# K and V of a cross-attention block as block products of two head groups, with another written order

## The chip, the cores and the metric

The kernel runs on one core of one Trainium2 chip. The metric is the device time in microseconds (us); before the change it is 765.32, the median of three runs (764.75 to 765.59). Engines are named as in the profile: PE (TensorE matmul) with its weight loads PEld, DVE (VectorE), ACT (ScalarE), POOL (GpSimd), SP (SyncE, which here only issues DMAs).

## The reference

One transformer block with cross attention, in f32, for 4 batches of 512 tokens, width 512, 16 heads of 32 and an MLP of 2048:

```python
x = layer_norm(hidden_states, ln1_w, ln1_b)
q = (x @ q_w + q_b).reshape(B, LQ, H, HD).transpose(0, 2, 1, 3)
k = (encoder_hidden_states @ k_w + k_b).reshape(B, LK, H, HD).transpose(0, 2, 1, 3)
v = (encoder_hidden_states @ v_w + v_b).reshape(B, LK, H, HD).transpose(0, 2, 1, 3)
scores = jnp.einsum('bhqd,bhkd->bhqk', q, k) * scale
scores = jnp.where(mask, scores, mask_value)
attn = jax.nn.softmax(scores, axis=-1)
out = jnp.einsum('bhqk,bhkd->bhqd', attn, v)
out = out.transpose(0, 2, 1, 3).reshape(B, LQ, D)
out = out @ cproj_w + cproj_b
hidden = out + residual
y = layer_norm(hidden, ln2_w, ln2_b)
y = jax.nn.gelu(y @ fc_w + fc_b, approximate=True)
y = y @ proj_w + proj_b
return residual + y
```

## The kernel before

The sixteen heads of a batch are taken as four groups of four heads; over the four batches there are 16 groups, w = 0 to 15. For each group PE makes K (`prep_k`, L422: four products of 128x512), Q (`prep_q`, L434: the same) and V (`prep_v`, L443: sixteen products of 128x128), each into one of the four accumulator banks of the ring `accs` (L253). ACT copies K and Q out with their bias, V without; POOL adds V's bias.

Then come four steps of 128 queries (qt = 0 to 3). `scores` (u, L458) writes one bank sc for each of the four heads; `exps` (x, L463) takes each bank with one DVE reduction (L469: mask and minimum) and one ACT exponential (L472). So the next u needs the four banks read by the four x before it. `turn` (r, L475) transposes 32x32 blocks on DVE; for each half of the queries `stay` (d, L494, POOL copies) and `exchange` (e, L501, DMAs issued by SP) bring them to the right partitions, and `attend` (a, L509) multiplies with V. `cproj` (c, L390) multiplies with the output weights, DVE adds the residual, POOL adds proj's bias (`prow`) into a second tile `hp`, and POOL issues the store of `hp` to DRAM (L400). The tile h itself is normalised in place for the MLP (`ln_norm`, L347).

The MLP already uses block products. `fc` (f, L574) takes 2x2 blocks of the weights and of y and forms them with seven block products in place of eight: sums of weight blocks by POOL (`w_sums`, L565, into two buffers `wsum`), sums of y by DVE (`y_sums`), and a chain in one bank to which PE adds three further products; between them ACT copies the bank's state (`joins`, L594: four copies of 128x256), and DVE adds the other bank's two halves (one add of 128x512, one of 128x256). proj (P, L703) does the same at two levels, with its sums on DVE (`pt`, `xs`, `gs`), and its results are added to the hidden state that `load_hid` reads back from DRAM (hd, L656; J, L739).

What sets the order is a text, `ORDER` (L61 to L216): each token names a function, its arguments stand behind colons, and each occurrence runs the function up to its next `yield`. Every engine runs its own instructions strictly in that order, and SP its DMA issues too. Weights of K, Q and V have two buffers for each kind (`kqv_w`, L312), taken by even and odd groups. Part of batch 0's MLP is written between the attention steps of groups 6 and later, and so on; all of proj stands behind the last attention step.

## Time and profile before

| | |
|---|---|
| median of three runs | 765.32 us (764.75 to 765.59) |
| the profiled execution: time, span | 765.16 us, 763.4 us |
| busy share of the span | PE 99%, PEld 71%, DVE 78%, ACT 52%, POOL 47% |
| granted TensorE clock | 1.00 of full speed |
| chain that ended last | PE 91%, DVE 3%, DMA 2%, ACT 2% |
| DMA | 157.45 MB, mean 206 GB/s |

Rows of the order of time read "start, length, engine, line, operation, out<-in, shape, xcount [idle before <- who ended it]". A row of groups has, behind the bar, the busy time in us and the mean length of one in ns, then the engine's idle time before it and what ended it. A row of waits reads "who <- on whom: us in total, times, longest". A row of stretches has a stretch, its length, and each engine's busy time in it with the number of its instructions. A product in f32 is two PE passes, so xcounts of PE are twice the products in the code. Lengths of PE rows include the pipeline's end; what a run of passes costs is read from one start to the next.

### The profile page before, as it was taken

How to read it: one execution, taken by the hardware profiler on the slowest of the kernel's cores; microseconds unless marked ns; L12 is line 12 of the kernel's file. 1: busy time of each engine (PE TensorE's matmuls, PEld its weight loads, DVE VectorE, ACT ScalarE, POOL GpSimd, SP SyncE). 2: the span in 40 equal slices, each digit the busy share in tenths (PEclk: the TensorE clock that was granted, in tenths of full speed). 3: DMA queues.
4: the chain of work that ended last, by engine and by line, in shares of the span. 5: the costliest groups of instructions: out<-in, count | busy, mean ns of one | idle time of the engine just before them, and what ended most of it. 6: DMA issues, size and time to landing. Idle time of an engine off the chain costs nothing.

```text
span 763.4 us, 14160 instructions
## 1 busy us (share of the span) xinstructions
PE 755.2 (99%) x4970; PEld 540.4 (71%) x4970; DVE 594.4 (78%) x1199; ACT 399.9 (52%) x948; POOL 359.5 (47%) x391
## 2 busy tenths in 40 slices
PE   9999999999999999999999999999999999999998
PEld 6556555466666556765665676766888999999997
DVE  3799988999778888887778886654778888867862
ACT  2567856446886686857867687741244221111110
POOL 1153744663577467644598656875302023231322
PEclk9999999999999999999999999999999999999999
DMA  8588888677678877478868777888445778589675
GB/s 288 176 228 238 208 213 225 181 218 208 166 215 226 229 249 206 151 202 235 222 185 216 220 241 235 231 261 304 151 139 181 219 207 190 128 193 282 127 145 110
DMA packets 69445, 157.45 MB, mean 206 GB/s; under 512 B 11600, under 2 KB 24272, under 8 KB 67712
## 3 DMA queue, kind: packets, MB, share of 16 engines
q1 hardware_dynamic: 54272, 126.72, 57.3%
q0 software_dynamic: 14960, 29.82, 16.0%
q8 instruction: 39, 0.64, 0.4%
q14 instruction: 30, 0.25, 0.1%
q10 hardware_dynamic: 144, 0.02, 0.0%
HBM read 69.23 MB, written 25.17 MB: 124 GB/s over the span
## 4 chain that ended last, share of the span: by engine, by line
PE 91%; DVE 3%; DMA 2%; ACT 2%; SPq 1%; issue 1%; POOL 0%; DVEq 0%; POOLq 0%; ACTq 0%
PE acc L572 37%; PE sc L572 12%; PE sc L461 8%; PE acc L426 7%; PE acc L438 7%; PE acc L448 7%; PE acc L519 6%; PE acc L393 6%; PE acc L361 2%; SPq L319 1%; DVE ptt L469 1%; DMA gd<-st 1%; ACT ptt L472 1%; PE acc L792 1%; DVE xn L354 0%
## 5 line engine op out<-in xcount | busy, mean ns | idle before, releaser
L472 ACT ACTIVATE ptt<-ptt,mn 128x512 f32<-128x512 f32 x256 | 183.0, 717 | 79.9 <-DVE mn L469 78.9
L469 DVE CUSTOM_DVE_ANT_0 ptt<-sc,mix 128x512 f32<-128x512 f32 x256 | 165.4, 678 | 35.9 <-PE sc L461 28.0
L497 POOL COPY swap<-swap 32x1088 f32<-32x1088 f32 x128 | 140.0, 1094 | 77.5 <-DVE swap L490 58.1
L480 DVE STREAM_TRANSPOSE swap<-ptt 128x1024 f32<-128x1024 f32 x64 | 79.1, 1235 | 9.3 <-ACT ptt L472 3.2
L487 DVE STREAM_TRANSPOSE swap<-ptt 128x1024 f32<-128x1024 f32 x64 | 78.3, 1223 | 0.0
L461 PE MATMUL sc<-pbt 32*128 32x512 f32 x512 | 74.9, 640 | 0.8 <-ACT pbt L440 0.8
L597 ACT COPY xn<-acc 128x128 f32<-128x128 f32 x75 | 18.5, 269 | 103.8 <-PE acc L572 102.8
L597 ACT COPY st<-acc 128x256 f32<-128x256 f32 x96 | 34.4, 368 | 71.2 <-PE acc L572 51.7
L620 POOL DMA_DIRECT2D gd<-st x32 | 23.5, 739 | 90.4 <-ACT st L618 61.8
L572 PE MATMUL acc<-ys,wsum 128*128 128x256 f32 x256 | 63.3, 384 | 1.2 <-ACT st L597 1.2
L448 PEld LDWEIGHTS acc<-ptt,ext 128*128 128x128 f32 x512 | 58.6, 192 | 7.6 <-issue 4.3
L448 PE MATMUL acc<-ptt,ext 128*128 128x128 f32 x512 | 60.7, 277 | 0.0
L519 PE MATMUL acc<-swap,mix 128*32 128x256 f32 x1024 | 60.6, 382 | 0.0
L426 PE MATMUL acc<-ext,ptt 128*128 128x512 f32 x128 | 58.4, 601 | 0.1
L438 PE MATMUL acc<-ext,ptt 128*128 128x512 f32 x128 | 58.5, 600 | 0.0
L572 PE MATMUL acc<-yT,pbt 128*128 128x256 f32 x240 | 57.9, 384 | 0.0
L393 PE MATMUL acc<-mix 128*128 128x512 f32 x128 | 57.7, 599 | 0.0
L572 PEld LDWEIGHTS acc<-ys,wsum 128*128 128x128 f32 x256 | 47.2, 190 | 14.0 <-ACT st L597 5.0
L572 PEld LDWEIGHTS acc<-yT,pbt 128*128 128x128 f32 x240 | 44.6, 190 | 16.4 <-issue 7.4
L519 PEld LDWEIGHTS acc<-swap,mix 128*32 128x32 f32 x1024 | 30.7, 110 | 32.4 <-issue 10.7
L322 DVE TENSOR_TENSOR st<-acc,st 128x512 f32<-128x512 f32 (+1 forms) x48 | 26.3, 547 | 31.1 <-ACT st L597 23.0
L472 ACT ACTIVATION_READ_ACCUMULATOR ptt<-ptt,mn 128x1 f32 x256 | 48.4, 189 | 0.0
(132 smaller groups left out, 1387.3 us busy)
## 6 DMA issues: line engine op xcount, KB each, us to landing
swap<-swap SPq DMA_DIRECT2D x384, 136.0 KB, 3.2
gd<-st POOLq DMA_DIRECT2D x32, 512.0 KB, 4.3
swap<-gd SPq DMA_DIRECT2D x12, 1024.0 KB, 7.5
pbt<-fc_w_dram SPq DMA_DIRECT2D x40, 256.0 KB, 3.7
xn<-x_dram SPq DMA_DIRECT2D x32, 256.0 KB, 4.3
ext<-fc_w_dram SPq DMA_DIRECT2D x24, 256.0 KB, 3.1
swap<-xn POOLq DMA_DIRECT2D x18, 256.0 KB, 5.3
ptt<-k_w_dram SPq DMA_DIRECT2D x16, 256.0 KB, 4.0
```

The lines of the kernel that those rows point to most:

```text
L393: nc.tensor.matmul(acc, oT[:, g, ts(t, P)], wc[:, g, :], start=(g == 0), stop=(g == NG - 1))
L426: nc.tensor.matmul(acc, S["wk", w][:, d, :], eT[:, d, :], start=(d == 0), stop=(d == ND - 1))
L438: nc.tensor.matmul(acc, S["wq", w][:, d, :], xT[:, d, :], start=(d == 0), stop=(d == ND - 1))
L448: nc.tensor.matmul(acc[:, ts(t, P)], eT[:, d, ts(t, P)], S["wv", w][:, d, :], start=(d == 0), stop=(d == ND - 1),)
L461: nc.tensor.matmul(sc[h], S["qT", w][r, ts(qt, P)], S["kT", w][r, :], start=True, stop=True)
L469: nc.vector.tensor_tensor_reduce(out=s, in0=sc[h], in1=mb, scale=1.0, scalar=FMAX, op0=ALU.add, op1=ALU.min, accum_out=mn)
L472: nc.scalar.activation(s, s, AF.Exp, bias=mn, scale=-1.0, accum_out=S["sums", w][:, qt, h : h + 1])
L480: nc.vector.transpose(*two_heads[0])
L487: nc.vector.transpose(*two_heads[1])
L497: nc.gpsimd.tensor_copy(pT[ts(i, HD), i], tb[ts(i, HD), i])
L519: nc.tensor.matmul(av[ts(h, HD), : 2 * P].rearrange(shape, **kw), v[:, t, ts(h, HD)], p[t][h], start=(t == 0), stop=(t == NT - 1),)
L572: nc.tensor.matmul(o, x[:, k], y[:, k], start=(k == 0 and not more), stop=(k == n - 1), skip_group_check=more)
```

## The change

K and V are made for a pair of groups p (groups 2p and 2p+1) at a time by fc's scheme: 2x2 blocks of the two groups' weights and 2x2 blocks of e (the transposed encoder states: two halves of the contraction, two halves of the tokens), seven block products (`kv`), sums of the weights (`kv_sums`, tokens ks and vs, four of 128x256) and of e (`e_sums`, token es, four of 128x512 for each batch) by POOL, and `joins` by ACT and DVE (tokens kj and vj; K's copies carry the bias). Groups 0 and 1 keep K as whole products (pk). V has two pair buffers in place of five single ones. The third sum of e and of the weights overwrites a block of its own input. The buffers of weight sums are a ring of two that K, V, fc and the last weight sums of proj share.

proj's bias is no longer added before the store: the store reads h, and `p_bias` (token pb) adds it by POOL to the hidden state that was read back, behind the attention; `load_row` (lr) loads its row over cproj's bias, which is done by then.

`ORDER` is another text throughout. In it, k:1 to k:4 and v:0 to v:3 stand whole ahead of u:7:0.

```diff
 ORDER = """
-s1:0 s1:0 s1:0 s1:0 r1:0 n1:0 k:0 lf:0:0 v:0 v:0 k:0 wv:2 wq:1 wv:1 k:1 n1:0 n1:0 n1:0 t1:0:1 t1:0:1 t1:0:0 t1:0:3
-  t1:0:0 t1:0:2 t1:0:2 m:0 qb t1:0:3 q:0 q:0
-u:0:0 x:0:0 x:0:0 x:0:0 x:0:0 q:1 r:0:0
-u:0:1 v:1 r:0:0 x:0:1 x:0:1 x:0:1 x:0:1 r:0:1
-u:0:2 r:0:1 r:0:1 x:0:2 v:2 x:0:2 k:1 r:0:1 x:0:2 v:2 x:0:2
...
+s1:0 s1:0 s1:0 s1:0 r1:0 pk:0 es:0 wk:2 pk:0 n1:0 n1:0 n1:0 n1:0 wv:1 wq:1 lx:1 vs:0 pk:1 t1:0:3 t1:0:0 t1:0:1 t1:0:3
+  t1:0:0 t1:0:2 t1:0:1 t1:0:2 q:0 v:0 m:0 qb s1:1 vs:0 vs:0 vs:0 es:0 es:0 es:0 q:0
+u:0:0 vj:0 x:0:0 x:0:0 x:0:0 v:0 x:0:0
+u:0:1 r:0:0 v:0 k:1 vj:0 x:0:1 v:0 x:0:1 pk:1 x:0:1 vj:0 x:0:1 r:0:0 r:0:1
+u:0:2 q:1 x:0:2 r:0:1 vj:0 kj:1 x:0:2 v:0 q:1 x:0:2 x:0:2 vj:0 r:0:1 r:0:1 r:0:2
+u:0:3 x:0:3 x:0:3 x:0:3 vj:0 x:0:3 lx:1 lf:0:0 lx:2 wq:2 lx:1 lx:1 lf:0:1 lf:0:3 wk:3 lc ks:1 m:0 ks:1 ks:1 wv:2 wq:3
+  wv:3 e:0:0 e:0:0 e:0:0 r:0:3 r:0:2 v:1 k:1 k:1
+u:1:0 kj:1 x:1:0 k:1 kj:1 x:1:0 r:0:3 x:1:0 q:3 q:3 vj:1 x:1:0 r:0:3
+u:1:1 ks:1 d:0:0 d:0:0 vs:1 vs:1 vs:1 r:0:3 d:0:1 vs:1 d:0:1 v:1 v:1 s1:1 x:1:1 kj:1 x:1:1 vj:1 k:1 kj:1 v:1 r:1:0
+  vj:1 s1:1 x:1:1 s1:1 x:1:1 r:1:0 r:1:1 kj:1 vj:1 q:2 r1:1 n1:1 n1:1 n1:1 q:2
+u:1:2 vb:0 v:1 a:0:0 wk:4 e:0:1 le:1 e:0:1 e:0:1 wk:5 le:1 le:1 lf:0:3 lh:0 r:1:1 r:1:1 x:1:2 x:1:2 wv:4 le:1 ks:2
+  es:1 vb:0 ks:2 vj:1 x:1:2 n1:1 vj:1 r:1:1 x:1:2
+u:1:3 ks:2 ks:2 es:1 es:1 r:1:2 x:1:3 a:0:0 d:1:0 t1:1:2 k:2 t1:1:1 x:1:3 t1:1:2 x:1:3 a:0:1 x:1:3
+u:2:0 r:1:2 r:1:3 a:0:1 r:1:3 kj:2 x:2:0 x:2:0 r:1:3 x:2:0 t1:1:0 k:2 k:2 kj:2 t1:1:0 t1:1:1 x:2:0
+u:2:1 k:2 t1:1:3 x:2:1 x:2:1 r:1:3 d:1:0 t1:1:3 e:1:0 e:1:0 e:1:0 wv:5 r:2:0 x:2:1 kj:2 d:1:1 vs:2 vs:2 es:1 wq:5 wq:4
+  e:1:1 e:1:1 x:2:1 a:1:0
+u:2:2 e:1:1 r:2:1 q:4 r:2:0 kj:2 x:2:2 x:2:2 x:2:2 r:2:1 k:2 kj:2 r:2:1 x:2:2 a:1:0 r:2:1
+u:2:3 wk:6 wq:6 d:1:1 d:2:0 vs:2 cb:0 vs:2 vb:1 wk:7 ks:3 ks:3 d:2:0 x:2:3 lf:0:2 e:2:0 e:2:0 q:5 wq:7 e:2:0 v:2 x:2:3
+  r:2:2 x:2:3 x:2:3 q:4 r:2:3 kj:2
...
     mix = const.tile([P, 33 * D // 2], F32, tag="mix", name="mix")
-    v_of = [mix[:, i * D : (i + 1) * D].rearrange("p (t f) -> p t f", t=NT) for i in range(5)]
-    mb = mix[:, 5 * D : 6 * D]
-    rr = mix[:, 6 * D : 6 * D + D // 2].rearrange("p (a h d) -> p a h d", a=2, h=HG)
-    wc, oT = (mix[:, 13 * D // 2 + i * ND * D : 13 * D // 2 + (i + 1) * ND * D].rearrange("p (d n) -> p d n", d=ND)
+    v_of = [mix[:, i * 2 * D : (i + 1) * 2 * D] for i in range(2)]
+    mb = mix[:, 4 * D : 5 * D]
+    rr = mix[:, 5 * D : 5 * D + D // 2].rearrange("p (a h d) -> p a h d", a=2, h=HG)
+    wc, oT = (mix[:, 11 * D // 2 + i * ND * D : 11 * D // 2 + (i + 1) * ND * D].rearrange("p (d n) -> p d n", d=ND)
               for i in range(2))
-    prow, hp = (mix[:, 29 * D // 2 + i * D : 29 * D // 2 + (i + 1) * D] for i in range(2))
+    es = mix[:, 27 * D // 2 : 33 * D // 2].rearrange("p (s i l) -> p s i l", s=3, i=2)
...
     yT = const.tile([P, ND, L], F32, tag="yT", name="yT")
     ys = const.tile([P, 3, 2, HL], F32, tag="ys", name="ys")
-    wsum = const.tile([P, 2, 3, 2, P], F32, tag="wsum", name="wsum")
+    wsums = Ring(const.tile([P, 3, 2, P], F32, tag=f"ws{i}", name=f"ws{i}") for i in range(2))
...
     def k_q(w, i):
-        n = w % 4 * 2 + i
-        return pbt[:, n * D : (n + 1) * D]
+        n = w // 2 % 2 * 4 + i * 2 + w % 2
+        return pbt[:, n * D : (n + 2 - i) * D]
...
         add(nc.vector, h, acc, h)
         accs.done("c", b, t)
         yield
-        add(nc.gpsimd, hp, h, prow)
-        nc.gpsimd.dma_start(out=xa[b][ts(t, P), :], in_=hp)
+        nc.gpsimd.dma_start(out=xa[b][ts(t, P), :], in_=h)
...
         return take
+    def bias(name, w):
+        k = {"k": KB, "q": QB}[name] + w % NG
+        return vec[:, k : k + 1]
+
     def prep_k(w):
-        kT = S["kT", w] = k_q(w, 0)
+
         acc = accs.take("k", w)
         for d in range(ND):
             nc.tensor.matmul(acc, S["wk", w][:, d, :], eT[:, d, :], start=(d == 0), stop=(d == ND - 1))
         yield
-        nc.scalar.activation(kT, acc, AF.Identity, bias=vec[:, KB + w % NG : KB + w % NG + 1], scale=1.0)
+        kT = S["kT", w] = k_q(w // 2 * 2, 0)[:, w % 2 * D : (w % 2 + 1) * D]
+        nc.scalar.activation(kT, acc, AF.Identity, bias=bias("k", w), scale=1.0)
         accs.done("k", w)
+
+    def e_blocks():
+        return [eT[:, 2 * k : 2 * k + 2, j * HL : (j + 1) * HL] for k in range(2) for j in range(2)]
+
+    def e_sums(b):
+        e = e_blocks()
+        return b_sums(nc.gpsimd, *e, es[:, 0], es[:, 1], e[1], es[:, 2])
+
+    def kv_sums(name):
+        def take(p):
+            a = [kqv_w(2 * p + i, "kqv".index(name)) for i in range(2)]
+            s = S["s" + name, p] = wsums.take(name, p)
+            return a_sums(nc.gpsimd, a[0][:, :2], a[0][:, 2:], a[1][:, :2], a[1][:, 2:], s[:, 0], s[:, 1], a[1][:, :2], s[:, 2])
+
+        return take
+
+    def kv(name):
+
+
+        def product(o, x, y, more=False):
+            for t in range(2 if name == "v" else 1):
+                for k in range(2):
+                    i, j = (y[:, k, ts(t, P)], x[:, k]) if name == "v" else (x[:, k], y[:, k])
+                    out_ = o[:, ts(t, P)] if name == "v" else o
+                    nc.tensor.matmul(out_, i, j, start=(k + t == 0 and not more), stop=(k == 1), skip_group_check=more or t > 0)
+
+        def take(p):
+            a, b = [kqv_w(2 * p + i, "kqv".index(name)) for i in range(2)]
+            e11, t3, e21, e22 = e_blocks()
+            t1, t2, t4 = (es[:, i] for i in range(3))
+            chain = S["qa", name, p] = accs.take("qa", name, p)[:, :HL]
+            product(chain, a[:, :2], e11)
+            yield
+            s = S["s" + name, p]
+            q = S["qc", name, p] = halves(accs.take("qc", name, p))
+            product(q[:, 0], a[:, 2:], e21)
+            product(q[:, 1], b[:, :2], t3)
+            yield
+            product(chain, s[:, 1], t2, True)
+            yield
+            product(chain, s[:, 0], t1, True)
+            yield
+            product(chain, s[:, 2], e22, True)
+            product(q[:, 1], b[:, 2:], t4, True)
+            wsums.done(name, p)
+
+        return take
+
+    def k_join(p):
+        kT = k_q(2 * p, 0)
+        for i in range(2):
+            S["kT", 2 * p + i] = kT[:, i * D : (i + 1) * D]
+        b = [bias("k", 2 * p + i) for i in range(2)]
+        return joins(kT.rearrange("p (i n) -> p i n", i=4), ("k", p), True, (b[0], b[0], b[1], b[1]))
+
+    def v_join(p):
+        v = v_of[p % 2]
+        for i in range(2):
+            S["v", 2 * p + i] = v[:, i * D : (i + 1) * D].rearrange("p (t f) -> p t f", t=NT)
+        return joins(v.rearrange("p (i n) -> p i n", i=4), ("v", p), True)
+
+    def v_bias(p):
+        for w in (2 * p, 2 * p + 1):
+            add(nc.gpsimd, S["v", w], S["v", w], row[:, 1, ts(w % NG, P)][:, None, :].broadcast_to([P, NT, P]))
+            yield
     def q_bias():
         nc.vector.tensor_scalar(qb, vec[:, QB : QB + NG], 0.0, -scale, ALU.add, ALU.mult)
...
         yield
         nc.scalar.activation(qT, acc, AF.Identity, bias=qb[:, w % NG : w % NG + 1], scale=-scale)
         accs.done("q", w)
-
-    def prep_v(w):
-        v = S["v", w] = v_of[w % 5]
-        acc = accs.take("v", w)
-        for t in range(NT):
-            for d in range(ND):
-                nc.tensor.matmul(
-                    acc[:, ts(t, P)], eT[:, d, ts(t, P)], S["wv", w][:, d, :],
-                    start=(d == 0), stop=(d == ND - 1),
-                )
-        yield
-        nc.scalar.copy(v, acc.rearrange("p (t f) -> p t f", t=NT))
-        accs.done("v", w)
-        yield
-        add(nc.gpsimd, v, v, row[:, 1, ts(w % NG, P)][:, None, :].broadcast_to([P, NT, P]))
...
         return [mlp_w(2 * (b * NP + c) + i) for i in range(2)]
     def fc_s(b, c):
-        s = wsum[:, c % 2]
+        s = S["sf", b, c]
         return s[:, 0], s[:, 1], fc_w(b, c)[1][:, :2], s[:, 2]
     def w_sums(engine, b, c):
         x, y = fc_w(b, c)
+        S["sf", b, c] = wsums.take("f", b, c)
         return a_sums(engine, x[:, :2], x[:, 2:], y[:, :2], y[:, 2:], *fc_s(b, c))
...
     def fc(b, c):
         a = fc_w(b, c)
         y11, t3, y21, y22 = y_blocks()
         t1, t2, t4 = (ys[:, i] for i in range(3))
-        s1, s2, s3, s4 = fc_s(b, c)
-
         chain = S["qa", b, c] = accs.take("qa", b, c)[:, :HL]
         product(chain, a[0][:, 0:2], y11)
         yield
+        s1, s2, s3, s4 = fc_s(b, c)
         q = S["qc", b, c] = halves(sc[c % HG] if b == LAST else accs.take("qc", b, c))
         product(q[:, 0], a[0][:, 2:4], y21)
         product(q[:, 1], s3, t3)
...
         yield
         product(chain, s4, y22, True)
         product(q[:, 1], a[1][:, 2:4], t4, True)
-
-    def joins(g, key, own):
+        wsums.done("f", b, c)
+
+    def joins(g, key, own, biases=None):
+
+        def copy(i):
+            if biases is None:
+                nc.scalar.copy(g[:, i], S["qa", *key])
+            else:
+                nc.scalar.activation(g[:, i], S["qa", *key], AF.Identity, bias=biases[i], scale=1.0)
         for i in (0, 2, 3):
-            nc.scalar.copy(g[:, i], S["qa", *key])
+            copy(i)
             yield
         q = S["qc", *key]
         add(nc.vector, g[:, 0:4:3], q, g[:, 0:4:3])
         yield
-        nc.scalar.copy(g[:, 1], S["qa", *key])
+        copy(1)
         accs.done("qa", *key)
         yield
         add(nc.vector, g[:, 2], q[:, 1], g[:, 2])
...
     def load_hid(b):
         for t in range(NT):
             load(hids[b % 2][:, t], xa[b][ts(t, P), :])
+            yield
+
+    def load_row():
+        load(row[:, 0, :], rows[1:2, :].broadcast_to([P, D]))
+
+    def p_bias(b):
+        for t in range(NT):
+            o = hids[b % 2][:, t]
+            add(nc.gpsimd, o, o, row[:, 0, :])
             yield
...
         nc.tensor.matmul(warm[:, :P], ident, ident, start=True, stop=True)
     accs.done("warm")
     load(row, rows[None, ::2, :].broadcast_to([P, 2, D]))
-    load(prow, rows[1:2, :].broadcast_to([P, D]))
     load_mask(0, nc.sync)
     takes = {
         "wk": load_k, "wq": load_q, "wv": load_v, "le": load_enc, "lc": lambda: load(wc, c_w),
-        "k": prep_k, "q": prep_q, "v": prep_v, "qb": q_bias, "m": make_mb,
+        "pk": prep_k, "q": prep_q, "es": e_sums, "k": kv("k"), "v": kv("v"), "ks": kv_sums("k"), "vs": kv_sums("v"),
+        "kj": k_join, "vj": v_join, "vb": v_bias, "lr": load_row, "pb": p_bias, "qb": q_bias, "m": make_mb,
...
```

The last weight sums of proj (pt:2) go through the ring in five subtractions in place of four. What is cut from the diff renames places in shared tiles.

More of the change, by code (lines that the diff above doesn't have):

```diff
@@ L571, in product @@
         for k in range(n):
-            nc.tensor.matmul(o, x[:, k], y[:, k], start=(k == 0 and not more), stop=(k == n - 1), skip_group_check=more)
+            w = y[k] if isinstance(y, list) else y[:, k]
+            nc.tensor.matmul(o, x[:, k], w, start=(k == 0 and not more), stop=(k == n - 1), skip_group_check=more)
     def fc(b, c):
@@ L686, in p_terms, with p_sums_split @@
         b11, b12, b21, b22 = quarters(p_of(n))
-        s = ws[n]
-        return (b11, b12, b21, b22), (s[:, 0], s[:, 1], ws3 if n == 4 else b12, s[:, 2])
-    def p_sums2(n):
-        b, t = p_terms(n)
-        return b_sums(nc.vector, *b, *t)
+        if n == 2:
+            t = [S["t2", i] for i in range(2)]
+            t1, t2 = ([w.rearrange("p s i n -> p (s i) n")[:, :4] for w in t])
+            t4 = [w[:, 2, i] for w in t for i in range(2)]
+        else:
+            t1, t2, t4 = ws[n]
+        return (b11, b12, b21, b22), (t1, t2, ws3 if n == 4 else b12, t4)
+    def p_sums2(n):
+        if n != 2:
+            b, t = p_terms(n)
+            return b_sums(nc.vector, *b, *t)
+        for i in range(2):
+            S["t2", i] = wsums.take("t2", i)
+        return p_sums_split()
+    def p_sums_split():
+        (b11, b12, b21, b22), (t1, t2, t3, _) = p_terms(2)
+        sub(nc.vector, t1, b12, b11)
+        yield
+        sub(nc.vector, t2, b22, t1)
+        yield
+        sub(nc.vector, t3, b22, b12)
+        yield
+        for i in range(2):
+            c = slice(2 * i, 2 * i + 2)
+            sub(nc.vector, S["t2", i][:, 2], b21[:, c], t2[:, c])
     def g_terms(b, n):
```

295 lines of the change are left out of this document (145 added, 150 removed).

## The prediction

> **What bounds the kernel now.** I read the page first, then the waits of PE and DVE, then the busy time by stretch, then the order of time for the prices.
>
> ```profile
> PE 755.2 (99%) x4970; PEld 540.4 (71%) x4970; DVE 594.4 (78%) x1199; ACT 399.9 (52%) x948; POOL 359.5 (47%) x391
> ...
> PE acc L792 <- POOL nhalf L781: 1.3, 1, 1.3
> PE acc L572 <- ACT st L597: 1.2, 1, 1.2
> PE acc L361 <- DVE xn L354: 1.0, 1, 1.0
> PE sc L461 <- ACT pbt L440: 0.8, 1, 0.8
> ```
>
> PE has no room: the list of its waits names 4.3 us in all. So time goes where PE's work goes, as long as no other engine takes over. The other engine to watch is DVE, and it must be read by stretch: from the first scores (u:0:0, 22.4) to those of group 7 (u:7:0, 198.9), from there to 490.0 (group 15's last scores), and behind.
>
> ```profile
> core 0: us, PE busy (x) PEld busy (x) DVE busy (x) ACT busy (x) POOL busy (x), PEclk, DMA share, GB/s
> 22.40:198.90 176.50, 175.39 (x1146) 96.88 (x1147) 162.25 (x357) 112.69 (x282) 88.09 (x90) 1.00 0.76 206
> 198.90:490.00 291.10, 289.75 (x1772) 183.73 (x1768) 233.90 (x501) 217.38 (x468) 187.11 (x211) 1.00 0.76 217
> 490.00:763.40 273.40, 269.82 (x1969) 245.98 (x1968) 191.09 (x325) 65.28 (x194) 82.29 (x83) 1.00 0.70 190
> ```
>
> The clock is full throughout (1.00). In the first stretch DVE is busy 162.25 of 176.50, 91.9%; in the second 80%, in the third 70%. In the first it is already nearly a second bound, because each scores group needs the four sc banks that DVE's reductions empty, and there is little MLP work yet to put between.
>
> **The change part by part.** The products of K and V. Prices are from start to start:
>
> ```profile
> 237.74 1.03 PE L572 MATMUL acc<-yT,wsum 128*128 128x256 f32 x4
> 238.60 1.03 PE L572 MATMUL acc<-ys,pbt 128*128 128x256 f32 x4
> ...
> 262.75 3.60 PE L426 MATMUL acc<-ext,ptt 128*128 128x512 f32 x8
> 266.18 1.03 PE L572 MATMUL acc<-ys,wsum 128*128 128x256 f32 x4
> ...
> 292.30 3.72 PE L572 MATMUL acc<-yT,pbt 128*128 128x256 f32 x16
> 295.85 1.03 PE L572 MATMUL acc<-ys,wsum 128*128 128x256 f32 x4
> ...
> 307.24 3.73 PE L448 MATMUL acc<-ptt,ext 128*128 128x128 f32 x32
> 310.81 3.60 PE L426 MATMUL acc<-ext,ptt 128*128 128x512 f32 x8
> ```
>
> A product stands in the trace as two passes. K of one group is 8 passes of 512 columns, 266.18 - 262.75 = 3.43, a pair 6.86. The new pair is 7 blocks of 2 products, 28 passes of 256 columns: at 238.60 - 237.74 = 0.86 for four that is 6.02, at 3.55 for sixteen 6.21. Seven of the eight pairs change (groups 0 and 1 keep whole products): -5.9, at worst -4.6. V of one group is 32 passes of 128 columns, 3.57, a pair 7.14; the new pair has 56, 6.25: -0.89 for each of 8 pairs, -7.1. Together **-13.0**. Each pair is issued in 5 runs in place of 2; the 64 scores groups stay as many, so I cost the breaks at nothing. If each of the 45 added runs paid 0.1 (what 16 passes in a row have over four times 0.86), -13.0 would be -8.5.
>
> ```profile
> L572 PEld LDWEIGHTS acc<-yT,pbt 128*128 128x128 f32 x240 | 44.6, 190 | 16.4 <-issue 7.4 <-ACT st L597 1.5 <-ACT st L618 0.8
> ```
>
> The new K has 196 passes, each with a load of 190 ns, where 112 stood: 84 more. The sixteen passes in 3.55, 222 ns each, already hold a load of 190 each, so loads hide beneath passes and I count nothing. The Trainium skill (TensorE: Matmul & The Clock Gate, Part 3, "What overlaps and what doesn't") says that a weight load runs beside matmuls in flight only if it goes to other row groups. These loads and passes all use the full 128 rows, so by that rule the 84 would add 16.0 and K would lose 10 instead of gaining 5.9; the trace differs, with 222 ns where load and pass one behind the other would take over 400.
>
> The head. What stands ahead of u:0:0 is set by x: its load, its statistics, the four normalisations of L354, transposes, q.
>
> ```profile
> 8.99 3.73 PE L448 MATMUL acc<-ptt,ext 128*128 128x128 f32 x32
> ...
> 12.56 3.60 PE L426 MATMUL acc<-ext,ptt 128*128 128x512 f32 x8
> ...
> 13.76 1.92 DVE L354 TENSOR_SCALAR xn<-xn,mv,rs 128x512 f32<-128x512 f32 x4 [1.45 <-POOL rs L341]
> ...
> 15.99 2.16 PE L361 MATMUL acc<-ident,xn 128*128 128x128 f32 x16
> ...
> 22.38 1.14 PE L461 MATMUL sc<-pbt 32*128 32x512 f32 x8 [0.78 <-ACT pbt L440]
> ```
>
> Before, V of group 0 (8.99 to 12.56) fills the wait. The new order has only V's first block there, 8 passes, 0.9; the other 2.7 is PE work that was free and now stands behind u:0:0: **+2.7**. The second K follows the first and may wait for its weights, but it is covered: before, it was done at 16.2, just as the transposes began.
>
> Beside it, POOL. After rs it was idle; now 8 sums of e and V stand there (four of 128x512, four of 128x256).
>
> ```profile
> 161.12 1.39 DVE L354 TENSOR_SCALAR xn<-xn,mv,rs 128x512 f32<-128x512 f32 x1
> 161.47 0.74 POOL L325 TENSOR_TENSOR wsum<-pbt,wsum 128x256 f32<-128x256 f32 x1
> 163.27 1.27 POOL L322 TENSOR_TENSOR mix<-xn,mix 128x512 f32<-128x512 f32 x1 [1.06 <-DMA xa<-mix]
> 163.37 1.45 DVE L354 TENSOR_SCALAR xn<-xn,mv,rs 128x512 f32<-128x512 f32 x1
> ```
>
> With POOL idle four of L354 take 1.92; beside a POOL sum one takes 1.39 to 1.45, as if it waited for the sum to end. On the head's chain that is 0 (sums late because their V weights land late) up to 4 x 0.9 = 3.6; I take **+2.0**, above the middle, since the sum of e needs no late load and begins as L354 does.
>
> The joins and the first stretch. Each of 15 products now ends in a join like fc's: four copies by ACT and two adds by DVE.
>
> ```profile
> L597 ACT COPY st<-acc 128x256 f32<-128x256 f32 x96 | 34.4, 368 | 71.2 <-PE acc L572 51.7 <-DMA gd<-st 19.4
> L428 ACT ACTIVATE pbt<-acc,vec 128x512 f32<-128x512 f32 x16 | 10.8, 677 | 7.1 <-PE acc L426 7.1
> L453 ACT COPY mix<-acc 128x512 f32<-128x512 f32 x16 | 9.1, 573 | 14.7 <-PE acc L448 14.6
> L322 DVE TENSOR_TENSOR st<-acc,st 128x512 f32<-128x512 f32 x24 | 16.4, 682 | 23.0 <-ACT st L597 23.0
> L322 DVE TENSOR_TENSOR st<-acc,st 128x256 f32<-128x256 f32 x24 | 9.9, 412 | 8.1 <-PE acc L572 8.1
> 24.15 0.69 DVE L469 CUSTOM_DVE_ANT_0 ptt<-sc,mix 128x512 f32<-128x512 f32 x1
> 24.76 0.69 DVE L469 CUSTOM_DVE_ANT_0 ptt<-sc,mix 128x512 f32<-128x512 f32 x1
> ```
>
> ACT: 4 x 0.368 = 1.47 a pair for 2 x 0.677 or 2 x 0.573; 15 pairs add some 3 us to an engine at 52%: nothing. DVE had no part in K and V. Instructions on it start 0.08 before the last ends (0.69 long, 0.61 apart), so a join costs 0.68 + 0.41 less 0.16, 0.94, and 15 cost 14. Behind u:7:0 DVE has 20% free and they cost nothing. Ahead of u:7:0 the new order has four K and four V pairs: PE's work there falls by 4 x 0.84 + 4 x 0.89 = 7.0, 176.5 to 169.5; DVE's rises by 8 x 0.94 = 7.5, 162.25 to 169.8. (Other work crosses the two ends, V of pair 4 to behind and MLP products to ahead; counted in the written order it about cancels on both engines.) DVE would have to be busy without a gap. Nothing in the trace shows it so over a long stretch; the largest of its waits there is this:
>
> ```profile
> DVE ptt L469 <- PE sc L461: 8.4, 8, 4.1
> ```
>
> As it falls behind PE, the 8.4 of waits for scores should go, and what is left of them all is a few us. Ends: 100% gives 169.8, +0.3 over PE's 169.5; the old 91.9% gives 184.8, +15.3. I take 97%, 175.0, **+5.5**, nearer the busy end because the largest wait is one that a late DVE doesn't have.
>
> PE's wait for a join: the third to fifth run adds to a bank that ACT must have copied first. fc has the same chain 32 times and PE waited 1.2 in all; 15 more, **+0.6** (0 to 15 x 1.2 = 18 if every one cost fc's longest).
>
> POOL: 60 sums for K and V and 16 for e.
>
> ```profile
> L325 POOL TENSOR_TENSOR wsum<-wsum,pbt 128x256 f32<-128x256 f32 x20 | 14.8, 746 | 0.2
> L322 POOL TENSOR_TENSOR mix<-xn,mix 128x512 f32<-128x512 f32 x16 | 20.5, 1284 | 25.8 <-issue 9.4 <-DMA xa<-mix 9.2 <-DVE xn L322 7.0
> SPq L319 <- PE acc L426: 10.2, 5, 7.6
> ptt<-k_w_dram SPq DMA_DIRECT2D x16, 256.0 KB, 4.0
> xa<-mix POOLq DMA_DIRECT2D x16, 256.0 KB, 3.3
> ```
>
> 60 x 0.746 + 16 x 1.284 = 65, so POOL goes from 359.5 to 424, 56%: nothing, at its share. If that cover fails (group 1 holds most: its sums and stays), what is late next is stay, then attend. proj's bias: the 16 adds of 1.284 leave the attention, where cproj's store waited for them, and come back behind it, where POOL is busy 82.29 of 273.40: nothing; uncovered in the last batch, 4 x 1.284 = 5.1. proj's row is loaded later by one DMA on SP in place of one in the head: nothing. But the store now reads h itself, which the normalisation overwrites in place, so DVE's first one of a batch waits until the store has landed, 3.3, with the reductions queued behind it and PE's scores behind those. Statistics (two steps) and POOL's rs stand between, so I take nothing; uncovered in all four batches it is 13.
>
> SP: a pair now uses both weight buffers of its kind, so the next pair's two loads wait for its last run, and the exchange DMAs queue behind them. A pair then needs its loads (4.0) and four sums (3.0) before the products, 7 us out of the 50 that two of the first seven groups take (176.5 x 2/7): nothing; if half of 7 pairs showed it, 25. Both sum buffers are shared with fc's sums in the same manner.
>
> The sum, against the profiled execution (765.16, span 763.4; the median of three is 765.32): 765.2 - 13.0 + 2.7 + 2.0 + 5.5 + 0.6 = **763.0**.
>
> **The rivals.** (a) DVE does not bind: the joins fit in its waits. Then +5.5 goes and 757.5 is left, without the contention in the head 755.5. For it: DVE's waits for scores vanish when it is late. Against: 169.8 of work in 169.5.
> (b) DVE keeps its old share in the first stretch, because its waits for ACT's exponentials and for transposes' buffers stay: 184.8, the time 772.8, slower. It decides at one point: 765.2 is reached at a stretch of 177.2, 169.8 / 177.2 = 95.8% busy; beneath 94.9% the kernel is slower by over 0.2%. For it: the row of 91.9%. Against: that row is of a DVE that waits for PE.
> (c) The change does not do what it says: PE's products shrink, but PE waits as long as they shrank, in the head and the first stretch (DVE at 95 to 96.5%): 764 to 766.9.
> (d) Loads of weights no longer hide: 16.0 more, 779. The sixteen passes in 3.55 speak against it.
>
> **How the numbers follow.** Over 0.2% (1.5 us) is what a measurement of this kernel can tell from no change. My forecast, 763.0 with 758 to 763.7 as its own range: 0.38. (a) 0.12. (c) 0.15. (b) 0.33. (d) 0.02. Faster is the forecast and (a), 0.50; the same (c), 0.15; slower (b) and (d), 0.35. The range of 8 in 10 runs from (a) without contention, 755.5, to just under (b), 772.5.
>
> **What would show it.** Right: L524 (scores) of u:7:0 starts some 5 us after a PE-bound 22 + 169.5, DVE busy 96 to 98% between; PE's list of waits gains scores that wait for DVE in that stretch and little behind it; u:0:0 starts near 24.5 with L363 longer than 0.54 each; passes of L467 keep 0.11 and 0.215. Wrong: waits of PE for ACT's copies or POOL's sums of many us, SP queued behind weights, or DVE under 95%.

## The result, and the profile after

The changed kernel takes 778.84 us (median of 777.04 to 780.34), against 765.04 for the kernel before on the same chip: a ratio of 1.0175, with a 95% interval of 1.0158 to 1.0193. Slower, and outside the range of the prediction (755.5 to 772.5). The profiled execution took 780.34, 1.5 above that median, with a span of 778.3, 14.9 more than the 763.4 of before.

The page of the changed kernel, busy time and granted clock in 40 slices:

```profile
PE 757.7 (97%) x4990; PEld 555.0 (71%) x4990; DVE 635.0 (82%) x1230; ACT 404.4 (52%) x978; POOL 426.6 (55%) x467
...
PEclk8999999999999999999999999999999999999999
```

PE was at 99% of the span and is at 97%. POOL stands where it was expected (424 predicted). DVE has 40.6 more than the 594.4 of before, and the joins explain some 14 of that (the forecast's price). So something else has made DVE's work longer. Busy time by the same three stretches (first scores, scores of group 7, last scores of group 15, end), changed kernel:

```profile
core 0: us, PE busy (x) PEld busy (x) DVE busy (x) ACT busy (x) POOL busy (x), PEclk, DMA share, GB/s
25.20:198.50 173.30, 171.52 (x1149) 101.95 (x1148) 165.81 (x371) 119.35 (x302) 115.88 (x128) 1.00 0.79 215
198.50:484.40 285.90, 285.39 (x1772) 187.96 (x1768) 239.12 (x509) 212.86 (x480) 196.66 (x224) 1.00 0.77 216
484.40:778.30 293.90, 280.39 (x2017) 253.41 (x2016) 219.68 (x332) 68.08 (x193) 104.08 (x99) 0.99 0.65 180
```

Against before (22.4, 176.5, 291.1, 273.4) the opening is 2.8 longer, the first stretch 3.2 shorter, the second 5.2 shorter, and the last 20.5 longer. The loss is behind attention, where none of the products that were changed runs; 5.3 of the 20.5 there is work of PE that the new order moved (worked out below), the rest is loss. PE's waits in the changed kernel, from the list of the whole span:

```profile
PE sc L637 <- DVE ext L334: 3.9, 1, 3.9
PE acc L438 <- DMA ptt<-k_w_dram: 3.5, 1, 3.5
PE sc L637 <- DVE xn L331: 2.1, 1, 2.1
PE sc L637 <- DVE st L331: 1.9, 1, 1.9
PE acc L893 <- POOL nhalf L882: 1.3, 1, 1.3
PE acc L637 <- DVE ws L334: 0.9, 1, 0.9
PE acc L637 <- DVE ext L334: 0.7, 2, 0.5
```

Five lines name DVE's additions and subtractions behind attention (9.5 us); before, the longest wait of PE was 1.3 and none was for these. The sums themselves, grouped by line and shape behind 484, changed kernel first (columns: count, then busy time and mean ns of one):

```profile
L334 DVE TENSOR_TENSOR ext<-swap 128x512 f32<-128x512 f32 x25 | 24.5, 985 | 0.0
L334 DVE TENSOR_TENSOR ext<-ext,swap 128x512 f32<-128x512 f32 x25 | 23.9, 958 | 0.7 <-PE sc L637 0.7
```

and the same sums before, behind 490:

```profile
L325 DVE TENSOR_TENSOR ext<-ext,swap 128x512 f32<-128x512 f32 x25 | 17.0, 684 | 0.1
L325 DVE TENSOR_TENSOR ext<-swap 128x512 f32<-128x512 f32 x25 | 17.0, 683 | 0.0
```

In these two groups the same instruction on the same shape takes 0.97 in the mean where it took 0.68. The longest of them, in order of time, changed kernel, DVE, POOL and PE:

```profile
694.23 5.00 DVE L334 TENSOR_TENSOR ext<-swap 128x512 f32<-128x512 f32 x1
...
694.49 1.72 POOL L331 TENSOR_TENSOR swap<-swap,row 128x512 f32<-128x512 f32 x1
695.70 1.67 POOL L849 DMA_DIRECT2D yT<-xn  x1
696.48 2.18 POOL L331 TENSOR_TENSOR swap<-swap,row 128x512 f32<-128x512 f32 x1
...
694.31 1.06 PE L637 MATMUL sc<-pbt,swap 128*128 128x128 f32 x8
699.28 1.16 PE L637 MATMUL sc<-pbt,ext 128*128 128x128 f32 x8 [3.92 <-DVE ext L334]
```

A subtraction of DVE lasts 5.00 us, from before the first bias addition of GpSimd (swap<-swap,row) until 0.57 behind the end of the second, and PE stands for 3.92 until it is done.

I counted DVE's instructions in the trace of the changed kernel: those with no GpSimd instruction beside them (DMA issues left aside), and those with a GpSimd addition at some moment of them (number, mean us, longest us). Those beside GpSimd's copies alone are in neither column.

```
                                            no GpSimd beside        beside an addition
two SBUF inputs, 128x512, add/subtract      146   0.686   0.697     21  1.909  5.000
two SBUF inputs, 128x256                     24   0.420   0.426      2  1.652  1.810
one PSUM, one SBUF input, 128x512            20   0.687   0.692     29  0.675  0.694
scores' reduction (PSUM, SBUF), 128x512      68   0.678   0.693    114  0.678  0.694
32x32 transposes, 128x1024                   25   1.224   1.246     68  1.225  1.246
normalisation (one SBUF input), 128x512      15   0.546   0.603      6  0.908  1.487
```

So GpSimd's additions do nothing to DVE's work in attention (PSUM inputs, transposes), and hold up the additions with two SBUF inputs, of which the projection's sums consist. The Trainium skill (SBUF — State Buffer, "Who interferes with whom") says that a DVE instruction with two SBUF inputs contends with a GpSimd instruction that reads SBUF, over a shared pair of ports that is an exclusive lock, and that issue order decides who blocks. The table agrees in that the rows with two SBUF inputs are hit and those with a PSUM input and the transposes are not; the normalisation, with one SBUF input, is hit as well. Two things in the row at 694.23 go beyond this rule. The subtraction was held over two GpSimd additions and not let in between them (so were those at 592.18 and 738.05, of 4.71 and 3.45; one at 726.83, of 3.85, was let in behind the first). And its record starts 0.26 ahead of the first of the two, which it yet gave way to; since GpSimd's records are rough, the trace can't tell which was issued first.

### The profile page after: what moved, and what is told of

The parts are those of the page before. It is cut to its first block, busy times and chain, and to the rows that moved or that the text cites. A ratio compares the mean times of both kernels' runs of the same rounds, so it can differ in the third digit from the quotient of the medians.

```text
span 778.3 us, 14426 instructions
## 1 busy us (share of the span) xinstructions
PE 757.7 (97%) x4990; PEld 555.0 (71%) x4990; DVE 635.0 (82%) x1230; ACT 404.4 (52%) x978; POOL 426.6 (55%) x467
## 4 chain that ended last, share of the span: by engine, by line
PE 69%; DVE 12%; issue 5%; DMA 5%; POOL 4%; ACT 2%; SPq 2%; DVEq 0%; POOLq 0%; ACTq 0%
PE acc L637 27%; PE sc L637 9%; PE acc L467 9%; PE sc L524 7%; PE acc L516 6%; PE acc L582 5%; PE acc L402 5%; SPq L328 2%; DVE ext L334 2%; DVE ptt L532 2%; DVE swap L543 1%; PE acc L370 1%; POOL swap L560 1%; DMA swap<-swap 1%; PE acc L438 1%
## 5 line engine op out<-in xcount | busy, mean ns | idle before, releaser
L663 ACT COPY st<-acc 128x256 f32<-128x256 f32 x128 | 46.0, 367 | 103.2 <-PE acc L637 84.3
L663 ACT COPY xn<-acc 128x128 f32<-128x128 f32 x100 | 23.5, 269 | 136.5 <-PE acc L637 134.5
L524 PE MATMUL sc<-pbt 32*128 32x512 f32 x512 | 78.0, 640 | 0.0
L691 POOL DMA_DIRECT2D gd<-st x32 | 23.7, 741 | 90.7 <-ACT st L689 56.9
L637 PE MATMUL acc<-ys,ws 128*128 128x256 f32 x256 | 65.4, 386 | 0.8 <-ACT st L663 0.7
L637 PEld LDWEIGHTS acc<-ys,ws 128*128 128x128 f32 x256 | 46.7, 190 | 18.2 <-issue 4.8
L516 PE MATMUL acc<-ext,ptt 128*128 128x512 f32 x128 | 58.4, 599 | 0.0
L849 POOL DMA_DIRECT2D swap<-xn x18 | 22.4, 1423 | 50.0 <-ACT xn L663 18.9
L689 ACT ACTIVATE st<-st,vec 128x512 f32<-128x512 f32 x64 | 43.6, 717 | 3.1 <-DVE st L331 2.7
L516 PEld LDWEIGHTS acc<-ext,ptt 128*128 128x128 f32 x128 | 23.5, 190 | 28.6 <-issue 23.5
L402 PEld LDWEIGHTS acc<-mix 128*128 128x128 f32 x128 | 23.6, 190 | 28.4 <-issue 26.3
```

Source lines behind the costliest of these rows:

```text
L402: nc.tensor.matmul(acc, oT[:, g, ts(t, P)], wc[:, g, :], start=(g == 0), stop=(g == NG - 1))
L516: nc.tensor.matmul(acc, S["wq", w][:, d, :], xT[:, d, :], start=(d == 0), stop=(d == ND - 1))
L524: nc.tensor.matmul(sc[h], S["qT", w][r, ts(qt, P)], S["kT", w][r, :], start=True, stop=True)
L637: nc.tensor.matmul(o, x[:, k], w, start=(k == 0 and not more), stop=(k == n - 1), skip_group_check=more)
L663: nc.scalar.copy(g[:, i], S["qa", *key])
```

## The experiments

The theories. A: the moved bias additions hold DVE up, by contention. B: they cost because the biased rows are now waited for (a load, an addition and then the joins, one behind the other). C: the new products of K and V, and the written order around them, lose the time. In the diffs below, a minus is the kernel named.

**The bias left out.** From the changed kernel:

```diff
-            add(nc.gpsimd, o, o, row[:, 0, :])
             yield
```

> The changed kernel without the 16 POOL adds of proj's bias behind the attention (the bias is left out of the result); the order and everything else stay. Theory A, the two engines' port: a DVE add or subtraction with both inputs in SBUF and a POOL add with both inputs in SBUF do not run side by side, so the 16 adds hold up DVE's sums and through them PE; without them the last stretch falls from 294 to about 279 and the time from 778.8 to about 765. Theory B, waiting in line: POOL's accumulating DMAs of proj's results stand behind adds that wait for the read-back of the hidden state; also about 765 here. Theory C, the written order of the last stretch itself (shared ring of sums, more MLP behind the attention): 777 to 779, no change.

Measured: 766.37 us, ratio to before 1.0019 [1.0000, 1.0039]. The last stretch takes 279.0 in place of 293.9. 12.5 of the 13.8 us are the 16 additions; C is left with the rest. A and B both forecast about 765 here, so this run doesn't part them.

**The bias added by VectorE.**

```diff
-            add(nc.gpsimd, o, o, row[:, 0, :])
+            add(nc.vector, o, o, row[:, 0, :])
```

> The changed kernel with the 16 adds of proj's bias made by DVE in place of POOL, at the same places of the order. Theory A: no POOL add is left to shut DVE out; DVE gets 16 x 0.61 = 9.8 more work in a stretch where it has room; about 766 to 769. Theory B: the accumulating DMAs no longer stand behind the adds on POOL, but DVE now waits for the read-back, with its sums queued behind: 770 to 778. Theory C: 777 to 780.

Measured: 766.03, ratio 1.0014 [0.9999, 1.0029]. The same rows, waited for in the same way, cost nothing that can be measured once VectorE adds them, although VectorE now has 16 more instructions. The two groups of sums that took 0.97 are back at 0.69 in this kernel, behind 484:

```profile
L334 DVE TENSOR_TENSOR ext<-ext,swap 128x512 f32<-128x512 f32 x25 | 17.1, 687 | 2.5 <-PE sc L637 2.5
L334 DVE TENSOR_TENSOR ext<-swap 128x512 f32<-128x512 f32 x25 | 17.1, 686 | 0.0
```

**The additions on GpSimd, on a tile that nobody waits for.** From the changed kernel, bias left out:

```diff
-            add(nc.gpsimd, o, o, row[:, 0, :])
+            add(nc.gpsimd, row[:, 1, :], row[:, 1, :], row[:, 0, :])
```

> The changed kernel with POOL's 16 adds at the same places, but onto a tile that nothing waits for (the row of V's bias, which is done by then), so they wait for no read-back and no accumulating DMA waits for their result; proj's bias is thus left out of the result. POOL's time and its two SBUF inputs stay. Theory A: the adds still shut DVE out, 774 to 779. Theory B: the waiting in line is gone, about 765 to 767. Theory C: 777 to 779.

Measured: 770.81, ratio 1.0080 [1.0057, 1.0102], between the forecasts of A and B. Contention alone costs 4.4 to 4.8 against the two kernels above; PE waits for DVE's sums up to 1.4 at a time, in place of 3.9. The 8 us up to the changed kernel come with the real rows: the additions then start when the rows land, and so beside other instructions of DVE. Whether the 8 is waiting in line or worse moments of contention, this run can't tell.

**The move alone.** The kernel before, with only proj's bias moved behind attention: `hp` and `prow` go, cproj's store reads h, `load_row` and `p_bias` are the changed kernel's, and their tokens (`lr`, sixteen `pb`) are added to an `ORDER` that otherwise stays:

```diff
-        add(nc.gpsimd, hp, h, prow)
-        nc.gpsimd.dma_start(out=xa[b][ts(t, P), :], in_=hp)
+        nc.gpsimd.dma_start(out=xa[b][ts(t, P), :], in_=h)
...
+            add(nc.gpsimd, o, o, row[:, 0, :])
```

> The kernel before with this part of the change alone: the store takes h itself, POOL's 16 adds of proj's bias stand behind the attention, each some 30 tokens behind the load of its tile. Theory A: DVE's sums of two SBUF inputs are shut out 16 times, of which a half to two thirds reach PE: 772 to 778 against 765.0. Theory B: 765 to 772, as far as the adds wait for loads. Theory C: 765 to 766.

Measured: 779.11, ratio 1.0178 [1.0162, 1.0194]. The move by itself, with the old products of K and V, makes as large a loss as the whole change (a little over A's range).

**The same additions aside, in the kernel before.** First on `hp`:

```diff
+    def p_aside(b):
+        for t in range(NT):
+            add(nc.gpsimd, hp, hp, prow)
+            yield
```

> The kernel before, with proj's bias where it was, and 16 more GpSimd additions of 128x512 on a tile that nobody reads, at the places behind attention where the changed kernel has its bias additions. Nothing waits for them and nothing else changes. Theory A, GpSimd shuts VectorE's two-operand additions out while it runs: 768.5 to 771, VectorE's additions there up to 2.5 us each, and the projection waits for them. Theory B, it is only the waiting in line for the biased rows that costs: 765 to 766, as before.

Measured: 777.82. It settles nothing: behind attention the space of `hp` and `prow` holds weight sums of the projection, so the additions changed those, waited for them and were waited for. Again, on the free half of the row tile:

```diff
-            add(nc.gpsimd, hp, hp, prow)
+            add(nc.gpsimd, row[:, 1, :], row[:, 1, :], row[:, 0, :])
```

> The kernel before with the same 16 GpSimd additions of 128x512 at the places behind attention, now on the second half of the row tile, which nobody reads there; the tile of the run before this one (777.82) turned out to be in use by the projection's sums, so that the additions held these up and were held up. Theory A, GpSimd shuts VectorE's two-operand additions out while it runs: 768.5 to 771.5, VectorE's additions there up to 2.5 us each. Theory B, only waiting in line for the biased rows costs: 765 to 766.5, as before.

Measured: 778.73, ratio 1.0169 [1.0144, 1.0195], far above what either theory was given. Sixteen additions that nobody reads cost as much as the moved bias (779.11): here waiting for rows has no part, and B falls. PE's waits and DVE's slowest group behind 484 of this kernel:

```profile
PE acc L574 <- DVE ext L327: 5.6, 2, 2.9
PE sc L574 <- DVE ext L327: 3.5, 3, 2.0
...
L327 DVE TENSOR_TENSOR ext<-swap,ext 128x512 f32<-128x512 f32 x25 | 21.8, 874 | 1.5 <-PE acc L574 1.3
```

The price was thought to be that of the run aside in the changed kernel, and is three times as large. The two kernels are written in another order; the same 16 additions, of 1.7 each, met other sums of DVE. The last stretch of the kernel without bias, of the run aside in the changed kernel, and of this one:

```profile
486.40:765.40 279.00, 275.08 (x2017) 250.03 (x2016) 194.86 (x332) 68.10 (x193) 81.26 (x83) 1.00 0.69 188
```

```profile
484.90:769.00 284.10, 276.35 (x2017) 250.04 (x2016) 213.20 (x332) 68.05 (x193) 103.93 (x99) 1.00 0.68 186
```

```profile
490.70:776.40 285.70, 273.00 (x1969) 247.76 (x1968) 208.38 (x325) 65.33 (x194) 105.78 (x99) 0.99 0.66 182
```

DVE is held up about as much in both: its busy time grows by 18.3 there (194.86 to 213.20) and by 17.3 here (191.09 before, 208.38). But PE's listed waits for DVE come to 3.9 there and 9.1 here. So what an addition costs depends on whether PE soon needs the sum that it meets, and isn't a constant.

**Each bias addition cut in four.** From the changed kernel:

```diff
-            add(nc.gpsimd, o, o, row[:, 0, :])
+            for i in range(4):
+                add(nc.gpsimd, o[:, ts(i, P)], o[:, ts(i, P)], row[:, 0, ts(i, P)])
```

> The changed kernel (778.84) with each of the 16 GpSimd bias additions of 128x512 cut in four of 128x128, in the same places. Theory L, a VectorE addition is shut out for as long as the GpSimd instruction that it met lasts: VectorE's additions meet pieces of 0.35 to 0.45 us, its longest fall from 5.0 us to under 2, and the time falls to 771 to 775. Theory S, the two share one path and what counts is the bytes that GpSimd moves: the longest stay above 3 us, and the time is 777.5 to 781, no better for the 48 more instructions.

Measured: 768.75, ratio 1.0039 [1.0015, 1.0062]: 10 us faster than the changed kernel, more than either theory gave, with the same bytes, the same places, and 48 more instructions on GpSimd (POOL is busy 119.00 of the last stretch in place of 104.08). So it isn't bytes, nor GpSimd's queue. And since the real rows are waited for here as in the changed kernel, waiting in line can hardly be more than 2.4 (768.75 less 766.37) of the 8 us that the run aside left open; the rest points to contention. DVE's 128x512 additions with two SBUF inputs that meet a GpSimd addition take 0.949 in the mean (31 of them), not 1.909. But the picture of one piece at a time is not exact either; the longest is 2.94 (a 128x1024, 1.22 alone), and this one of 128x256 (0.42 alone) waits through all four pieces, DVE and POOL in order of time:

```profile
565.38 2.22 DVE L334 TENSOR_TENSOR ws<-ws,ext 128x256 f32<-128x256 f32 x1
565.54 1.76 POOL L331 TENSOR_TENSOR swap<-swap,row 128x128 f32<-128x128 f32 x4
567.52 0.41 DVE L331 TENSOR_TENSOR ws<-ext 128x256 f32<-128x256 f32 x1
```

**The joins' additions left out.** From the kernel with the bias on VectorE, for the part that is left to C:

```diff
-        add(nc.vector, g[:, 0:4:3], q, g[:, 0:4:3])
+        if not kv_:
+            add(nc.vector, g[:, 0:4:3], q, g[:, 0:4:3])
...
-        add(nc.vector, g[:, 2], q[:, 1], g[:, 2])
+        if not kv_:
+            add(nc.vector, g[:, 2], q[:, 1], g[:, 2])
```

> The kernel with proj's bias added by VectorE (766.03), without the two VectorE additions of each of the K and V joins: the second and third blocks of K and V lack their cross products. It takes some 14 us of work off VectorE and nothing off TensorE. Theory D, VectorE bounds the first stretch of attention (the prediction's third step): that stretch falls from 175.4 to 169 to 171 and the time to 760.5 to 762.5. Theory W, the gain of the K/V part went into a handful of separate waits of TensorE (weights, layer norm, ScalarE's copies of the joins), and its scores never wait for VectorE: that stretch falls by at most 1.5, the time is 764.5 to 766.5.

Measured: 765.72, ratio 1.0008 [0.9986, 1.0029], 0.3 from its base and within its noise. The first stretch, of the base and of this kernel:

```profile
23.70:199.10 175.40, 171.91 (x1147) 102.26 (x1147) 166.00 (x371) 119.69 (x302) 116.09 (x128) 1.00 0.79 213
```

```profile
23.70:195.70 172.00, 170.62 (x1149) 101.52 (x1148) 159.15 (x355) 118.80 (x302) 115.80 (x128) 1.00 0.79 217
```

DVE has 6.85 less to do and the stretch is 3.4 shorter (1.8 against the run without bias, whose stretch is 173.8), between the two forecasts; the time followed theory W. (The additions left out go into the first, third and fourth of the four blocks, not the second and third.) DVE slows that stretch in part, but doesn't bound it: it falls to 92.5% busy and the rest stays. Theory W isn't right to the letter either. Scores do wait for DVE inside their runs, where the list of waits doesn't see it: in the changed kernel four of the 28 groups of scores in this stretch take 1.82 to 2.11 from their first pass to the end of their last, most of the others 1.14.

```profile
114.68 1.14 PE L524 MATMUL sc<-pbt 32*128 32x512 f32 x8
119.38 2.11 PE L524 MATMUL sc<-pbt 32*128 32x512 f32 x8
```

From start to next pass that is some 2 us more over the stretch than before, where two groups are long.

**The opening.** In the changed kernel's opening, DVE and PE in order of time, the second K waits for weights:

```profile
4.91 3.61 PE L438 MATMUL acc<-ext,ptt 128*128 128x512 f32 x8
11.98 6.71 PE L438 MATMUL acc<-ext,ptt 128*128 128x512 f32 x8 [3.47 <-DMA ptt<-k_w_dram]
18.53 2.13 PE L370 MATMUL acc<-ident,xn 128*128 128x128 f32 x16
...
13.76 3.67 DVE L363 TENSOR_SCALAR xn<-xn,mv,rs 128x512 f32<-128x512 f32 x4 [1.45 <-POOL rs L350]
```

Its eight passes take 6.71 in place of 3.61: over 8 to 20 us the granted clock is 0.72. So the loads were put in another order, from the kernel with the bias on VectorE:

```diff
     load_k(0)
...
+    load_k(1)
     load_v(0)
     for _ in load_x((1, 0)):
         pass
-    load_k(1)
     load_q(0)
```

> The kernel with proj's bias added by VectorE (766.03), and the load of the second K weights issued ahead of the first V weights, so that K of head group 1 does not wait for its weights behind K of group 0 (2.8 us in that run, and about 2.1 us more because the eight passes behind the wait ran at half clock). Theory H, the opening lost what the K/V part gained there: the first scores start at 21.5 to 22.5 us instead of 23.7, and the time falls by 1 to 2.5, to 763.5 to 765. Rival: x's rows now land behind the second K weights, layer norm comes later, and the scores start no earlier: 765.5 to 766.5.

Measured: 771.28, ratio 1.0077 [1.0055, 1.0100], slower by 5 and outside both forecasts. The wait of K is gone, and the transposes wait instead, for a layer norm whose x now lands behind two weights:

```profile
5.35 7.57 PE L438 MATMUL acc<-ext,ptt 128*128 128x512 f32 x16
16.90 0.48 PE L370 MATMUL acc<-ident,xn 128*128 128x128 f32 x1 [3.98 <-DVE xn L363]
```

The first scores start at 27.3, not 23.7, which is 3.6 of the 5; the rest isn't placed. In the next, two of GpSimd's sums over the encoder move ahead of layer norm as well:

```diff
-s1:0 s1:0 s1:0 s1:0 r1:0 pk:0 es:0 wk:2 pk:0
+s1:0 s1:0 s1:0 s1:0 es:0 es:0 r1:0 pk:0 wk:2 pk:0
```

> The kernel before in this list (second K weights early), and the first two of GpSimd's four sums over the encoder blocks written ahead of layer norm's first statistics, so that fewer of them run while VectorE normalises x. If GpSimd's sums stretch the normalisations (0.94 to 1.49 us each in the opening against about 0.54 alone), these come to 0.55 to 0.95, the transposes start up to 1 us earlier, and the time is 0.3 to 1 below that kernel's. If the transposes wait for the second K anyway, the same as that kernel within 0.5.

Measured: 769.92, ratio 1.0058 [1.0046, 1.0070], 1.4 lower, but the two intervals overlap, so the gain is not shown; the scores start at 26.9. Last, from this kernel, with V's weights behind everything:

```diff
-    load_k(1)
-    load_v(0)
     for _ in load_x((1, 0)):
         pass
+    load_k(1)
     load_q(0)
+    load_v(0)
```

> The kernel with proj's bias added by VectorE (766.03), with the opening's loads in the order K 0, encoder, x, K 1, Q 0, V 0 (there: K 0, encoder, V 0, x, K 1, Q 0) and two of the encoder's sums ahead of layer norm. In the run with K 1 ahead of V 0 and of x (771.28) the scores started at 27.3 us, since x landed behind both and layer norm with it. If the opening is bound by the order of these loads, x lands one weight earlier than in either, the scores start at 21 to 22.5 us instead of 23.7, and the time is 763 to 765. If V 0, now last, is late for its sums and product, the first stretch of attention grows by what the opening gains: 765.5 to 767.

Measured: 765.19, ratio 1.0001 [0.9983, 1.0018]. The scores start at 21.3, as the first theory said, with K's wait down to 1.49:

```profile
10.89 3.70 PE L438 MATMUL acc<-ext,ptt 128*128 128x512 f32 x8 [1.49 <-DMA ptt<-k_w_dram]
...
21.26 1.14 PE L524 MATMUL sc<-pbt 32*128 32x512 f32 x8
```

Of the 2.4 that the opening gained, the median shows 0.8, within its interval, and just over the first theory's 765. It is the best version with the new K and V, and can't be told from the kernel before.

## Why the prediction was wrong

**The step that failed** is the one on proj's bias: "the 16 adds of 1.284 leave the attention … and come back behind it, where POOL is busy 82.29 of 273.40: nothing; uncovered in the last batch, 4 x 1.284 = 5.1." It asked whether POOL had room and who waits for POOL. It didn't ask what a POOL addition does to DVE. In the last stretch PE's undisturbed passes rose by 5.3 (work that the new order moved there), and the excess of passes over that rose from 0.8 to 15.9: 10.7 of waits for DVE (counted from start to start; the list gives 9.5), and some 3.6 more of slow passes, most of them where the granted clock fell, behind the wait of 3.92 at 695 us and that of 1.86 at 602. Behind the one of 2.07 at 731 it stayed full:

```profile
600.00:620.00 20.00, 18.14 (x129) 17.25 (x129) 15.33 (x24) 5.21 (x15) 2.66 (x3) 0.91 0.60 211
700.00:720.00 20.00, 20.00 (x167) 20.00 (x167) 14.52 (x25) 2.83 (x13) 2.38 (x2) 0.91 0.63 163
720.00:740.00 20.00, 17.93 (x161) 17.74 (x160) 17.01 (x19) 2.60 (x11) 9.39 (x8) 1.00 0.51 110
```

In attention the additions had been harmless, because DVE's work there is on PSUM inputs and transposes, which the table above shows untouched. Rows that could have priced the move stood in the trace of before, behind its last scores, where the last batch's additions of GpSimd still run and sums of the MLP and the projection begin to mix in:

```profile
528.98 1.27 POOL L322 TENSOR_TENSOR xn<-xn,row 128x512 f32<-128x512 f32 x1
...
529.53 1.27 DVE L325 TENSOR_TENSOR ptt<-pbt 128x512 f32<-128x512 f32 x1
...
539.22 1.46 POOL L322 TENSOR_TENSOR mix<-xn,mix 128x512 f32<-128x512 f32 x1 [1.03 <-DMA xa<-mix]
539.45 1.77 DVE L325 TENSOR_TENSOR ptt<-pbt,ptt 128x512 f32<-128x512 f32 x1
```

Six of 170 such DVE additions met a GpSimd one before; they took 1.09 in the mean, the others 0.684. The prediction read the group's mean, which hides six, and used the same effect only for the normalisation in the opening ("1.39 to 1.45, as if it waited for the sum to end"). The rivals failed likewise: none had this mechanism. That rival (d), weight loads no longer hidden, came to 779 is a coincidence: the loads stayed hidden (see the next paragraph), and without the 16 additions the time is 766.4.

**K's and V's products, −13.0.** By price this was right: the passes of both traces, counted at 0.112, 0.216 and 0.429 each, come to 609.4 before and 596.4 without the moved bias. It also costs next to nothing to break them up: a pass ahead of scores or attend takes 0.094 more, but 63 times before and 70 now, 0.7, not 45 x 0.1. Loads of weights stayed hidden, as counted. Yet without the bias's contention the kernel stands 0.5 to 0.9 above before (766.03 and 766.37 against 765.49 in the same set of runs), where the other terms of the sum gave 2.2 below.

**The opening, +4.7.** The changed kernel's scores start at 25.2 ("near 24.5"). But a part of the reason given was wrong: "the second K … may wait for its weights, but it is covered". It waits 3.5, runs at a low clock behind that, and ends at 18.5, 1.1 behind the last normalisation. Those took 3.67 for four where 1.92 was the row of before, 1.75 for the +2.0 forecast, but in this run K, and not they, held the transposes. So the forecast start came near partly by luck.

**The first stretch, 175.0.** It took 173.3 here, and 173.8 and 175.4 in the kernels without the bias and with it on VectorE; DVE was 95.7% busy, between the 97% forecast and the 95% named as the mark of an error. That the length came so near is in part luck, since DVE's work there was 165.81 and not 169.8. The mechanism holds in part only: with DVE's join additions gone it was still 172.0, though PE's passes would allow some 168 (176.5 less 8.7 of products, plus 0.4 of breaks). What keeps it there is, by the trace of the kernel with the bias on VectorE, some ten separate waits of PE of 0.2 to 1.0 (Q's weights 0.9, ACT's copies 0.6 twice, the normalisations of the next batch 0.3 four times, others) and four groups of scores that wait for DVE's reductions inside their runs (3 us in all, against 1 before), not one bound.

**Waiting for the joins' copies, +0.6; SP and the paired buffers, nothing; the store that reads h, nothing.** No such wait is long in the trace: the list names 0.7, 0.4 and smaller for ACT, and none for SP's weights but those of the opening and, in two of the runs, of Q. Together, rival (c) describes the K and V part as it came out (766.0 and 766.4, in its 764 to 766.9): the products shrank, and PE waited about as long as they shrank. By spans, the kernel with VectorE's bias lost against its price 4.0 in the opening, 7.2 in the first stretch, 2.8 in the second and 1.6 in the last. That profiled execution was 2.5 slower than its median, so these are upper values, and the split among single waits wasn't tested one by one.

## What to carry to other kernels

Before work is moved onto an engine with idle time, look at what its neighbours do at the new place: in these traces a GpSimd addition is free beside DVE instructions that read PSUM (0.675 to 0.678 beside one), and holds up, for its whole length and more, those with two SBUF inputs (up to 5.00 in place of 0.69). Price it from the single rows where the two meet in the trace, not from a group's mean, and prefer DVE itself for the addition where the projection's sums run on DVE (766.0 against 778.8 here), or short GpSimd pieces (768.8). Products that are 13 us cheaper gain nothing if the order around them turns the gain into waits, so the waits should be costed by place as well as the products.

## What the runs showed of the hardware

- The same 16 GpSimd additions cost 4 to 5 us in one order and 13 in another, though nobody read their result and DVE was held up about as long. GpSimd's own records stretched too: 1.70 and 2.14 for the bias additions (means of 8 each) where 1.28 was the mean of 16 before.
- A DVE addition that meets GpSimd is not always let in when GpSimd's instruction ends: 5.00 us over two additions with a DMA issue between them, 2.22 over four pieces in a row. Cutting the instructions still won back 10 of 13.
- Behind two of the three longest waits of PE in the last stretch (3.92 and 1.86) the granted clock was 0.91 over a stretch of 20 us, with 1.6 to 1.7 of slow passes each; behind the third (2.07) it was 1.00. What parts them, no run here shows.
